# A selective scan, its projections and its convolution issued over twice as many elements, and the D * x term moved from TensorE to VectorE

## The chip, the core and the metric

One NeuronCore of a Trainium2 chip runs the whole program. The metric is the device time of one execution in microseconds (us). The engines named below are PE (TensorE, matrix multiply), DVE (VectorE), ACT (ScalarE), POOL (GpSimd) and SP (SyncE, which only issues DMAs here). Each works through its own instructions in order; semaphores tie them together.

## The reference

`x` is 8 sequences of 1024 tokens of 512 features, all float32. It is normalized, and two branches of the normalized `xn` are added to it:

```
xn  = layernorm(x)
out = x + mamba(xn) + ffn(xn)

mamba:  xb, z   = split(xn @ W_in)                        # 1024 channels each
        xc      = silu(causal_conv4(xb) + conv_b)         # depthwise, 4 taps
        B, C, d = split(xc @ W_x)                         # 16, 16, 1
        dt      = softplus(d + dt_bias)
        h_t     = h_{t-1} * exp(dt_t * A) + dt_t * xc_t * B_t      # 16 states a channel
        y_t     = sum over states(h_t * C_t) + D * xc_t
        result  = (y * silu(z)) @ W_out

ffn:    silu(q(xn) @ q(w_gate)) * (q(xn) @ q(w_up)), quantized, @ q(w_down)
```

Here `q` is a blockwise FP4 quantize and dequantize in blocks of 16, and the hidden width of `ffn` is 1408.

## The kernel before

**Chunks and slots.** Tokens are taken in chunks of `T` = 512: 16 chunks, two per sequence, so every even chunk starts from a zero state (`first`) and every odd one continues its neighbour and hands nothing on (`last`). The 1024 channels are 8 blocks `j` of 128. For the scan the 128 partitions hold 32 channels times 4 states, so a block is 4 quarters of channels (`NQ`), and the 16 states are 4 groups `q` (`NG`). A pair is one `(c, j, q, h)` with `h` the first of two neighbouring quarters: 64 pairs a chunk, 1024 in all. The loop in `sweep` gives each pair one slot.

**What one pair does.** `make_u` (L496): POOL multiplies `dt * x` by `B` for both quarters, 128x1024, into one of 3 `u` buffers, two slots ahead. `make_a` (L503): ACT computes `exp(dt * A)`, one instruction per quarter because the scale differs, into one of 2 PSUM buffers `ah`, one slot ahead. `scan` (L512): DVE runs the recurrence in place, one `tensor_tensor_scan` of 512 elements per quarter (L518), keeps the last column in `state` when the next chunk needs it (L524), and multiplies both quarters by `C` into one of 4 buffers `hc` (L526). Every two slots `sum_states` (L529) lets PE add the 4 states of a channel group into the PSUM bank `py`: 8 matmuls with the constant `summed`. At `q == 0` a 128x128 matmul with the diagonal `Dd` puts `D * xc` into `py` first (L535), with `xc` read back from DRAM as `xcr` (`fetch_x`, L546). After the last group `gate` (L555) multiplies `py` by `silu(z)`, read back as `zr` (`fetch_z`, L551).

**What runs beside it.** `sweep` (L821) fills PE with three other streams, written as generators that yield a cost in us: `ahead` (L471) prepares chunk `c + 1`, `finish` (L579) multiplies chunk `c - 1` by `W_out`, and `gate_up` (L600) or `downs` (L730) is the feed-forward. A credit per slot spreads the remaining cost evenly over the remaining slots, but for the last 12. The first sweep covers chunks 0 to 9 (640 slots) with `gate_up`, the second chunks 10 to 15 (384 slots) with `downs`. In both, the order on every engine is the order of the Python calls.

**Projection and convolution.** `project_x` (L337) multiplies 128 channels in two halves of 256 tokens, each with 3 tokens before it (259 columns, from an `xT` tile that holds 3 more tokens than the chunk), so that each half carries what its convolution needs. `convolve` reads the bank four times on ACT: one Identity with bias and scale (L351) and three scaled copies, `taps` (L357). `add` sums the taps on POOL (L363). `project_z` (L370) is 512 columns wide and is copied by ACT. `silus` (L386) follows when four halves are convolved; if they are not, it is put off by a slot.

**Work that follows later.** `later` (L272) puts an item into the list of a later slot, and `issue` (L279) takes the items of a slot in order. An item waits for the next slot if ACT work of `ENOUGH` = 2.0 us or more is already taken in this one, or if an item with the same key was put off.

**Banks.** Three PSUM banks (`p_mm`) serve all projections. They are used in a ring: `room` (L305) lets a new one start only if the last but two has had its reader issued:

```python
return whose in self.partly or len(self.banks) < 3 or not self.banks[-3][1]
```

The functions that the change touches:

Of the kernel before, what the change touches and what calls it, by code (L numbers as in the profile page):

```python
# [17 lines left out]
P = 128  # L18
# [6 lines left out]
LEAST = math.log(1.05 * 2.0**22)  # L25
T = 512
# [10 lines left out]
MOST = 6.0  # L37
TAIL = 12
# [47 lines left out]
class Net:  # L86
# [11 lines left out]
    def __init__(self, tc, ctx, x, W_in, conv_w, conv_b, W_x, A_log, D_param, dt_bias, W_out,  # L98
# [22 lines left out]
        self.p_mm = ctx.enter_context(tc.tile_pool(name="p_mm", bufs=3, space=PSUM))  # L121
# [35 lines left out]
        self.cb, self.dtb, Dp = vecs  # L157
# [12 lines left out]
        nc.vector.tensor_scalar(self.A, self.A, -1.0, None, ALU.mult)  # L170
# [7 lines left out]
        self.Dd = cpool.tile([P, J, P], F32, tag="Dd", name="Dd")  # L178
        for j in range(J):
            nc.vector.tensor_scalar(self.Dd[:, j, :], ident, Dp[:, j : j + 1], None, ALU.mult)  # L180
# [4 lines left out]
    def transposed(self, pp, src, n, name):  # L185
# [3 lines left out]
        for k0 in range(0, n, 4):  # L189
            kn = min(4, n - k0)  # L190
            pt = self.p_mm.tile([P, 4, P], F32, tag="mm", name=f"pt_{name}_{k0}")
            for k in range(kn):
                nc.tensor.transpose(pt[:, k, :], src[:, (k0 + k) * P : (k0 + k + 1) * P], self.ident)
            nc.scalar.copy(st[:, k0 : k0 + kn, :], pt[:, :kn, :])
        return st
# [83 lines left out]
    def issue(self):  # L279
# [3 lines left out]
        while self.due.get(self.now):  # L283
            item = work, bank, key, act = self.due[self.now].pop(0)
            if key in [i[2] for i in kept] or (act and used >= ENOUGH and self.timed):
                kept.append(item)
                continue
            used += act
            work()
            for b in bank or ():  # L290
                b[1] = False
# [7 lines left out]
    def bank(self, shape, name):  # L299
        assert self.room()  # L300
        b = [self.p_mm.tile(shape, F32, tag="mm", name=name), True]
        self.banks.append(b)
        return b

    def room(self, whose=None):  # L305

        return whose in self.partly or len(self.banks) < 3 or not self.banks[-3][1]
# [8 lines left out]
    def begin(self, c):  # L316
# [3 lines left out]
        H0 = self.H0  # L320
        s.xT = self.pool.tile([P, self.KM, H0 + T], F32, tag="xT", name=f"xT_{c}", bufs=1)
        if s.first:
            nc.gpsimd.memset(s.xT[:, :, :H0], 0.0)
        else:
            nc.sync.dma_start(s.xT[:, :, :H0], self.xnT_d[c - 1][:, :, T - H0 :])
        nc.sync.dma_start(s.xT[:, :, H0:], self.xnT_d[c])
        s.xc = self.pool.tile([P, self.J, T], F32, tag="xc", name=f"xc_{c}", bufs=1)
        s.z, s.xz_d, s.dd_d, s.reps = {}, [None] * self.J, [None] * self.J, [None] * self.J
        s.B, s.C, s.active, s.convolved = [None] * NG, [None] * NG, 0, 0
# [7 lines left out]
    def project_x(self, s, j, i, w):  # L337

        nc, c, H0 = self.nc, s.c, self.H0
        TH = T // 2  # L340
        b = self.bank([P, T], f"px_{c}_{j}_{i}")
        px = b[0]
        for k in range(self.KM):
            nc.tensor.matmul(  # L344
                px[:, : H0 + TH], w[:, k, :], s.xT[:, k, i * TH : i * TH + H0 + TH],
                start=(k == 0), stop=(k == self.KM - 1),
# [631 lines left out]
```

## Time and profile before

| | |
|---|---|
| median of 3 runs | 5353.9 us (5351.65 to 5355.68) |
| the profiled execution | 5357.3 us, of which the span of its instructions is 5355.5 us |
| preparation, up to the first scan | 0 to 537 us |
| first sweep, chunks 0 to 9 | 537 to 3745 us, 5.01 us a slot |
| second sweep, chunks 10 to 15 | 3745 to 5322 us, 4.11 us a slot |
| last output projection | 5322 to 5355 us |

Busy time is the time an engine spent in instructions; it overlaps between engines. A group of the profile lists a line, its engine, output <- inputs, the shape, the count, then busy us and the mean ns of one, then how long the engine stood idle just before such instructions and what ended that. The trace has two records for each float32 matmul of the program (one for each transpose). PEclk is the share of full speed that the clock of TensorE was granted. The ends of matmuls are modelled, so for them busy time divided by the count says more than the mean of one.

### The profile page before, as it was taken

How to read it: one execution, taken by the hardware profiler on the slowest of the kernel's cores; microseconds unless marked ns; L12 is line 12 of the kernel's file. 1: busy time of each engine (PE TensorE's matmuls, PEld its weight loads, DVE VectorE, ACT ScalarE, POOL GpSimd, SP SyncE). 2: the span in 40 equal slices, each digit the busy share in tenths (PEclk: the TensorE clock that was granted, in tenths of full speed). 3: DMA queues.
4: the chain of work that ended last, by engine and by line, in shares of the span. 5: the costliest groups of instructions: out<-in, count | busy, mean ns of one | idle time of the engine just before them, and what ended most of it. 6: DMA issues, size and time to landing. Idle time of an engine off the chain costs nothing.

```text
span 5355.5 us, 57041 instructions
## 1 busy us (share of the span) xinstructions
PE 4465.9 (83%) x17604; PEld 2529.2 (47%) x17604; DVE 4601.1 (86%) x5094; ACT 3312.6 (62%) x4829; POOL 4110.3 (77%) x2474
## 2 busy tenths in 40 slices
PE   3433788888898988989888998986998999899975
PEld 2322555564555556555555655654433343434321
DVE  3678789888898888788888888889899999899997
ACT  4665576766767577565767767576555565556532
POOL 6666788887888788787888988888677777778654
PEclk7765899999999999989999999998999999999986
DMA  5465557565665657556575665757586878587752
GB/s 158 142 206 155 148 172 192 148 193 153 178 185 154 188 139 204 152 161 177 162 201 157 190 176 157 192 148 212 156 241 162 228 194 236 160 229 195 220 128 57
DMA packets 635584, 937.83 MB, mean 175 GB/s; under 512 B 58624, under 2 KB 378112, under 8 KB 635152
## 3 DMA queue, kind: packets, MB, share of 16 engines
q1 hardware_dynamic: 624880, 931.66, 62.9%
q10 hardware_dynamic: 10400, 2.52, 0.2%
q8 instruction: 141, 2.31, 0.2%
q14 instruction: 163, 1.34, 0.1%
HBM read 676.81 MB, written 257.20 MB: 174 GB/s over the span
## 4 chain that ended last, share of the span: by engine, by line
PE 36%; DVE 31%; ACT 11%; POOL 8%; issue 8%; DMA 5%; SPq 1%; DVEq 0%; ACTq 0%; POOLq 0%
DVE ah L518 19%; PE pu L625 7%; PE po L589 6%; PE pod L748 6%; PE pg L625 5%; DVE hc L526 5%; PE pz L375 3%; ACT ah L507 3%; PE py L537 3%; POOL u L498 2%; PE px L344 2%; ACT L507 1%; POOL xc L363 1%; DVE pu L649 1%; PE ps L411 1%
## 5 line engine op out<-in xcount | busy, mean ns | idle before, releaser
L498 POOL TENSOR_TENSOR u<-rep,B 128x1024 f32<-128x1024 f32 x1024 | 2413.0, 2360 | 776.1 <-DVE ah L518 736.5
L507 ACT ACTIVATE ah<-rep,A 128x512 f32<-128x512 f32 x2048 | 1416.6, 692 | 1406.8 <-DVE hc L526 1359.3
L518 DVE TENSOR_TENSOR_SCAN ah<-ah,state,u 128x512 f32<-128x512 f32 x1024 | 1313.4, 1283 | 33.1 <-ACT ah L507 12.4
L526 DVE TENSOR_TENSOR hc<-ah,C 128x1024 f32<-128x1024 f32 x1024 | 1249.6, 1220 | 95.1 <-PE py L537 53.8
L518 DVE TENSOR_TENSOR_SCAN ah<-ah,u 128x512 f32<-128x512 f32 x1024 | 1254.0, 1225 | 44.2 <-ACT ah L507 21.6
L625 PE MATMUL pu<-wu,xq 128*128 128x256 f32 (+1 forms) x3072 | 683.9, 380 | 85.5 <-DVE h L640 25.3
L625 PE MATMUL pg<-wg,xq 128*128 128x256 f32 (+1 forms) x3072 | 661.0, 373 | 58.8 <-DMA wg<-gu 13.7
L537 PE MATMUL py<-hc,summed 128*32 128x512 f32 x4096 | 618.6, 629 | 80.8 <-DVE hc L526 80.5
L625 PEld LDWEIGHTS pu<-wu,xq 128*128 128x128 f32 x3072 | 564.5, 199 | 231.1 <-issue 29.3
L748 PE MATMUL pod<-dT,hTr 128*128 128x512 f32 x1408 | 637.6, 603 | 24.3 <-DMA hTr<-hT 19.0
L625 PEld LDWEIGHTS pg<-wg,xq 128*128 128x128 f32 x3072 | 557.0, 196 | 183.6 <-issue 74.8
L363 POOL TENSOR_TENSOR xc<-xc,taps 128x256 f32<-128x256 f32 x768 | 558.1, 727 | 82.5 <-ACT taps L357 42.3
L344 PE MATMUL px<-xT,wx 128*128 128x259 f32 x2048 | 530.1, 407 | 94.0 <-ACT h L636 47.9
L375 PE MATMUL pz<-xT,wz 128*128 128x512 f32 x1024 | 511.6, 646 | 71.1 <-ACT z L382 32.0
L344 PEld LDWEIGHTS px<-xT,wx 128*128 128x128 f32 x2048 | 393.9, 199 | 282.3 <-ACT taps L357 69.5
L589 PE MATMUL po<-Wout,y 128*128 128x512 f32 x1024 | 465.3, 607 | 13.5 <-ACT hT L678 10.0
L748 PEld LDWEIGHTS pod<-dT,hTr 128*128 128x128 f32 x1408 | 261.1, 191 | 398.5 <-issue 360.8
L375 PEld LDWEIGHTS pz<-xT,wz 128*128 128x128 f32 x1024 | 205.4, 207 | 330.3 <-issue 215.8
L589 PEld LDWEIGHTS po<-Wout,y 128*128 128x128 f32 x1024 | 192.5, 193 | 281.3 <-issue 262.6
L357 ACT ACTIVATE taps<-px,cw 128x256 f32<-128x256 f32 x768 | 305.5, 472 | 12.9 <-POOL xc L363 12.8
L640 DVE TENSOR_TENSOR h<-h,pu 128x512 f32<-128x512 f32 x192 | 121.8, 637 | 220.0 <-PE pu L625 216.5
L537 PEld LDWEIGHTS py<-hc,summed 128*32 128x32 f32 x4096 | 88.4, 109 | 437.6 <-issue 205.0
(107 smaller groups left out, 4482.1 us busy)
## 6 DMA issues: line engine op xcount, KB each, us to landing
rep<-ddd SPq DMA_DIRECT2D x512, 512.0 KB, 7.1
ddd<-dd SPq DMA_DIRECT2D x128, 512.0 KB, 4.4
hTr<-hT SPq DMA_DIRECT2D x64, 704.0 KB, 4.9
wg<-gu SPq DMA_DIRECT2D x80, 512.0 KB, 5.6
wu<-gu SPq DMA_DIRECT2D x80, 512.0 KB, 5.9
hT<-hT SPq DMA_DIRECT2D x80, 512.0 KB, 6.2
wx<-in_L_attn_W_in_dram SPq DMA_DIRECT2D x128, 256.0 KB, 2.8
wz<-in_L_attn_W_in_dram SPq DMA_DIRECT2D x128, 256.0 KB, 3.0
```

The source lines that it names most:

```text
L344: nc.tensor.matmul(px[:, : H0 + TH], w[:, k, :], s.xT[:, k, i * TH : i * TH + H0 + TH], start=(k == 0), stop=(k == self.KM - 1),)
L357: nc.scalar.activation(taps[:, k, :], px[:, k : k + TH], AF.Copy, scale=self.cw[:, j, k : k + 1])
L363: nc.gpsimd.tensor_tensor(ca, ca, taps[:, k, :], ALU.add)
L375: nc.tensor.matmul(b[0], w[:, k, :], s.xT[:, k, self.H0 :], start=(k == 0), stop=(k == self.KM - 1))
L498: self.nc.gpsimd.tensor_tensor(u, s.reps[j][:, h : h + 2, 1, :], s.B[q].unsqueeze(1).to_broadcast([P, 2, T]), ALU.mult)
L507: self.nc.scalar.activation(ah[:, i, :], s.reps[j][:, h + i, 0, :], AF.Exp, scale=self.A[:, g, q : q + 1])
L518: nc.vector.tensor_tensor_scan(ah[:, i, :], ah[:, i, :], u[:, i, :], 0.0 if s.first else self.state[:, g + i, q : q + 1], ALU.mult, ALU.add,)
L526: nc.vector.tensor_tensor(hc, ah, s.C[q].unsqueeze(1).to_broadcast([P, 2, T]), ALU.mult)
L537: nc.tensor.matmul(s.py[i * D4 : (i + 1) * D4, :], self.summed, hcs[i // 2][:, i % 2, :], start=False, stop=(q == NG - 1),)
L589: nc.tensor.matmul(b[0], s.y[:, j, i * P : (i + 1) * P], self.Wout[:, j, :], start=(j == 0), stop=(j == self.J - 1),)
L625: nc.tensor.matmul(b[0][:, i, :], xq[pair][:, k, i * P : (i + 1) * P], w[:, k, :], start=(k == 0), stop=(k == self.KM - 1),)
L748: nc.tensor.matmul(b[0], h[:, k, :], dT[:, k, :], start=(k == 0), stop=(k == self.KF - 1))
```

## The change

- **One scan per pair.** Both quarters go through one scan of 1024 elements. The decay at the first token of the second quarter must then be zero: `separate` (ACT) overwrites that `dt` with 1e30 so that its exp is 0, after it has computed that token's decay for all 4 groups into `carry`. For an odd chunk, `make_a` adds `carry * state` to the first element of the second quarter's `u` with one 128x1 Identity on ACT.
- **512 tokens at once.** `project_x` is one group of 4 matmuls of 512 columns. `convolve` reads its bank four times at 512 columns. `add` shifts the taps on POOL by slices; what reaches into the next chunk is kept in `over` and added there. `xT` no longer holds the 3 tokens before.
- **D * x at the gate.** DVE adds `xr * D` to `py` in place with `scalar_tensor_tensor`, ahead of the multiplication by `zr`. `Dd`, its matmul and `fetch_x` go; `fetch_xz` reads both `xr` and `zr` at the place where `zr` was read.
- **Any free bank.** The banks carry numbers; a new projection takes the one that was given back longest ago, in whatever order that came.
- Around these, `silus` and the copy of `z` return `AGAIN` when they are not ready and are then kept for the next slot; the keys of `add` and of the copy of `z` are their own. The costs that the sweep reckons with follow: 64 for `ahead` instead of 68, 1.1 for the first sum instead of 2.0.

The diff, cut to its core:

```diff
-        self.p_mm = ctx.enter_context(tc.tile_pool(name="p_mm", bufs=3, space=PSUM))
+        self.p_mm = ctx.enter_context(tc.tile_pool(name="p_mm", bufs=1, space=PSUM))
...
-        nc.vector.tensor_scalar(self.A, self.A, -1.0, None, ALU.mult)
+        nc.vector.tensor_scalar(self.A, self.A, -1.0, -SLOW, ALU.mult, ALU.min)
...
     def bank(self, shape, name):
-        assert self.room()
-        b = [self.p_mm.tile(shape, F32, tag="mm", name=name), True]
-        self.banks.append(b)
-        return b
+        i = self.frees.pop(0)
+        return [self.p_mm.tile(shape, F32, tag=f"mm{i}", name=name), i]
 
     def room(self, whose=None):
-        return whose in self.partly or len(self.banks) < 3 or not self.banks[-3][1]
+        return whose in self.partly or bool(self.frees)
...
+            if work() is AGAIN:
+                kept.append(item)
+                continue
             used += act
-            work()
             for b in bank or ():
-                b[1] = False
+                self.frees.append(b[1])
...
-    def project_x(self, s, j, i, w):
+    def project_x(self, s, j, w):
...
-                px[:, : H0 + TH], w[:, k, :], s.xT[:, k, i * TH : i * TH + H0 + TH],
-                start=(k == 0), stop=(k == self.KM - 1),
+                px, w[:, k, :], s.xT[:, k, :], start=(k == 0), stop=(k == self.KM - 1)
...
-            taps = self.pool.tile([P, H0, TH], F32, tag="dd", name=f"taps_{c}_{j}_{i}")
+            taps = []
             for k in range(H0):
-                nc.scalar.activation(
-                    taps[:, k, :], px[:, k : k + TH], AF.Copy, scale=self.cw[:, j, k : k + 1]
-                )
+                if k % 2 == 0:
+                    tile_ = self.pool.tile([P, 2, T], F32, tag="dd", name=f"taps_{c}_{j}_{k}")
+                taps.append(tile_[:, k % 2, :])
+                nc.scalar.activation(taps[k], px, AF.Copy, scale=self.cw[:, j, k : k + 1])
             def add():
+                over = self.over[:, j, :]
+                tt = nc.gpsimd.tensor_tensor
                 for k in range(H0):
-                    nc.gpsimd.tensor_tensor(ca, ca, taps[:, k, :], ALU.add)
+                    tt(ca[:, H0 - k :], ca[:, H0 - k :], taps[k][:, : T - H0 + k], ALU.add)
+                if not s.first:
+                    tt(ca[:, :H0], ca[:, :H0], over, ALU.add)
+                if not s.last:
+                    nc.gpsimd.tensor_copy(over, taps[0][:, T - H0 :])
+                    for k in range(1, H0):
+                        tt(over[:, : H0 - k], over[:, : H0 - k], taps[k][:, T - H0 + k :], ALU.add)
                 s.convolved += 1
-            self.later(1, add, key="a")
-        self.later(1, convolve, [b], "a", 2.2)
+            self.later(1, add, key="c")
+        self.later(1, convolve, [b], "a", 2.8)
...
         def copy():
+            if i == 0 and s.stored < h:
+                return AGAIN
...
-        self.later(1, copy, [b], "a", 0.6)
+        self.later(1, copy, [b], "z", 0.6)
...
-        if s.convolved < 4 * (h + 1):
-            self.later(1, lambda: self.silus(s, h), None, "a", 4.7)
-            return
+        if s.convolved < 2 * (h + 1) or s.copied < 2 * (h + 1):
+            return AGAIN
...
+    def separate(self, s, j):
+        nc = self.nc
+        if not s.first:
+            v = s.carry[j] = self.pool.tile(
+                [P, NQ // 2, NG], F32, tag="carry", name=f"carry_{s.c}_{j}"
+            )
+            for i in range(NQ // 2):
+                nc.scalar.activation(
+                    v[:, i, :], self.A[:, j * NQ + 2 * i + 1, :], AF.Exp,
+                    scale=s.reps[j][:, 2 * i + 1, 0, 0:1],
+                )
+        nc.scalar.copy(s.reps[j][:, 1::2, 0, 0], self.long)
...
     def make_a(self, s, j, q, h):
+        if q == h == 0:
+            self.separate(s, j)
...
+        if not s.first:
+            first = self.us[len(self.ahs)][:, 1, 0:1]
+            nc.scalar.activation(
+                first, self.state[:, j * NQ + h + 1, q : q + 1], AF.Identity, bias=first,
+                scale=s.carry[j][:, h // 2, q : q + 1],
+            )
...
-        for i in range(2):
-            nc.vector.tensor_tensor_scan(
-                ah[:, i, :], ah[:, i, :], u[:, i, :],
-                0.0 if s.first else self.state[:, g + i, q : q + 1],
-                ALU.mult, ALU.add,
-            )
+        a = ah.rearrange("p i t -> p (i t)")
+        nc.vector.tensor_tensor_scan(
+            a, a, u.rearrange("p i t -> p (i t)"),
+            0.0 if s.first else self.state[:, g, q : q + 1], ALU.mult, ALU.add,
+        )
...
-            nc.tensor.matmul(s.py, self.Dd[:, j, :], s.xcr, start=True, stop=False)
...
-        if q == 0 and j + 1 < self.J:
-            self.later(1, lambda: self.fetch_x(s, j + 1))
...
-        self.nc.vector.tensor_tensor(s.y[:, j, :], s.py, s.zr, ALU.mult)
+        v = self.nc.vector
+        v.scalar_tensor_tensor(s.py, s.xr, self.Dp[:, j : j + 1], s.py, ALU.mult, ALU.add)
+        v.tensor_tensor(s.y[:, j, :], s.py, s.zr, ALU.mult)
         if j + 1 < self.J:
-            self.later(1, lambda: self.fetch_z(s, j + 1))
+            self.later(1, lambda: self.fetch_xz(s, j + 1))
...
-        left = cost + len(now) // per * (29.0 + 68.0 + sums)
+        left = cost + len(now) // per * (29.0 + 64.0 + sums)
...
-                left -= 1.1 if pq else 2.0
+                left -= 1.1
```

## The prediction

> **What bounds the kernel now.** I read the busy shares first, then a table of engine times by stage, then what DVE and PE waited for in the first sweep, and last a stretch of the timeline where nothing but the scan is left. The page's totals:
>
> ```profile
> PE 4465.9 (83%) x17604; PEld 2529.2 (47%) x17604; DVE 4601.1 (86%) x5094; ACT 3312.6 (62%) x4829; POOL 4110.3 (77%) x2474
> ```
>
> No engine is full over the span. By stage (first sweep, second sweep, the end of the second without other PE work):
>
> ```profile
> 537.00:3745.00 3208.00, 2790.57 (x12248) 1788.57 (x12248) 2755.98 (x2944) 2144.47 (x3094) 2654.69 (x1596) 0.94 0.62 172
> 3745.00:5322.00 1577.00, 1436.34 (x4464) 574.77 (x4464) 1489.99 (x1468) 843.18 (x1285) 1109.11 (x661) 0.94 0.69 187
> 5180.00:5322.00 142.00, 65.25 (x154) 7.89 (x152) 135.89 (x113) 47.67 (x69) 78.02 (x34) 0.56 0.26 63
> ```
>
> Columns: stretch, length, PE, PEld, DVE, ACT, POOL, granted clock, DMA share, GB/s. The second sweep is DVE's: 1490 of 1577 us. In the first, DVE has 2756 and PE 2791 of 3208 us, and they wait for each other. DVE's waits there, and some of PE's:
>
> ```profile
> DVE h L640 <- PE pu L625: 216.5, 74, 28.5
> DVE r_False L576 <- PE po L589: 64.4, 20, 9.3
> DVE hc L526 <- PE py L537: 46.2, 22, 4.8
> DVE ah L518 <- ACT ah L507: 27.2, 28, 3.9
> ```
>
> ```profile
> PE px L344 <- ACT h L636: 47.9, 10, 8.9
> PE pth L675 <- ACT h L636: 40.9, 17, 9.2
> PE px L344 <- ACT taps L357: 37.3, 18, 7.0
> ```
>
> DVE stands for PE 335 us in all (the three rows and three of 4.1, 3.1 and 0.5), because PE is late with results that stand ahead of the next scan in DVE's order. PE stands some 310 us for readers (ACT mostly) that must empty a bank or finish an input. So DVE's work plus DVE's waits for PE make the first sweep, and DVE's work alone most of the second.
>
> **The scan.** At the end of the second sweep a slot is bare:
>
> ```profile
> 5256.48 1.23 DVE L526 TENSOR_TENSOR hc<-ah,C 128x1024 f32<-128x1024 f32 x1
> 5257.62 2.61 DVE L518 TENSOR_TENSOR_SCAN ah<-ah,state,u 128x512 f32<-128x512 f32 x2
> 5260.33 1.23 DVE L526 TENSOR_TENSOR hc<-ah,C 128x1024 f32<-128x1024 f32 x1
> ```
>
> Scan to scan is 3.86 us; two scans take 2.61 with `state`, and 2.50 in a zero-start chunk. These groups price the parts:
>
> ```profile
> L507 ACT ACTIVATE ah<-rep,A 128x512 f32<-128x512 f32 x2048 | 1416.6, 692 | 1406.8 <-DVE hc L526 1359.3
> L518 DVE TENSOR_TENSOR_SCAN ah<-ah,state,u 128x512 f32<-128x512 f32 x1024 | 1313.4, 1283 | 33.1 <-ACT ah L507 12.4
> L526 DVE TENSOR_TENSOR hc<-ah,C 128x1024 f32<-128x1024 f32 x1024 | 1249.6, 1220 | 95.1 <-PE py L537 53.8
> L518 DVE TENSOR_TENSOR_SCAN ah<-ah,u 128x512 f32<-128x512 f32 x1024 | 1254.0, 1225 | 44.2 <-ACT ah L507 21.6
> L344 PE MATMUL px<-xT,wx 128*128 128x259 f32 x2048 | 530.1, 407 | 94.0 <-ACT h L636 47.9
> L375 PE MATMUL pz<-xT,wz 128*128 128x512 f32 x1024 | 511.6, 646 | 71.1 <-ACT z L382 32.0
> ```
>
> No row has a scan of 1024. The step from 512 to 1024 elements is seen in `y` (L558, 128x512 out of PSUM, 682 ns) against `hc` (1220 ns): two short ones cost 2 x 682 - 1220 = 144 ns more than one long. A long scan is then 2 x 1225 - 144 = 2306 ns from zero, 0.19 us under 2.50, and 1283 + 1225 - 144 = 2364 ns with `state`, 0.25 under 2.61. Even and odd chunks are equal in number: 0.22 a slot. Bounds: nothing (all cost is by element), and 0.30, if the fixed part is a whole tiny copy (L524, 163 ns) besides the start from `state` (58 ns) and a gap of 0.08. A loss I leave out, since `hc` already crosses the same two banks in one instruction, its second 512 elements at 538 ns. I take 0.22, nearest to the `y` and `hc` rows: **141 us** off DVE in the first sweep (640 slots), **84** in the second (384); bounds 0 and 192, 0 and 115.
>
> **The gate.** One `scalar_tensor_tensor` of 128x512 per block comes to DVE. On two columns this form (L248, median 156 ns) costs what a copy does (163), so I take 0.70 from the `y` row; bounds 0.68 and 1.29 (the slowest row of 512, a scan). 80 blocks in the first sweep: +56 (54 to 103); 48 in the second: +34 (33 to 62). The single bank `py` is held 0.70 longer; the next block's first sum comes two slots later, so its cover is some 7 us of scans; without it PE would lose up to 90 us in all. `xr` is fetched eight slots ahead. The SP queue keeps the number of these reads; the eight small `xT` reads go.
>
> **PE.** `Dd` goes: group L535 is 140.2 us in 128 blocks, 1.10 each. Of the projections, 530.1 becomes 1024 records at `pz`'s 0.50 = 512, so 0.14 a block. First sweep 80 blocks: -99; second: -59. The weight loads that go ran beside matmuls: nothing. On PE alone this frees no time; it counts through DVE's waits. To size that I took the compiled order of both kernels, cut PE's list at each group of sums (512 stretches of two slots, 320 in the first sweep) and priced each stretch by busy time per matmul from the groups of before (`pg`, `pu` 0.43, `pz` 1.00, `po`, `pod`, `ps` 0.91, a sum 0.30, and so on). In the first sweep a stretch lasts 10.0 us on average; PE work beyond that is 368 us in all, close to DVE's 335 us of waits for PE (91%). Afterwards the first sweep's list is more even, since two halves became one group and banks come back in any order: stretches over 13.2 us fall from 45 to 14. At 9.5 us a stretch (where the sum below ends) the excess is 267, which at 91% is 243 us: **-92**. Bounds: 0, and -250 (PE's bank waits mostly gone). It leaves PE without other work in the last 20 slots of that sweep, where DVE sets the pace. In the second sweep DVE's waits for PE are 40 us, and the excess falls by a tenth: -4.
>
> The trace grants 0.94 of the clock in both sweeps but 0.56 where PE is busy 46%. [...]
>
> **ACT.** Convolution: six taps (305.5 / 768 = 0.40 each) and two L351 (0.55) are 3.5 us a block; three and one at 512 columns, 0.214 more each (`h` L636: 596 against 382 ns), are 2.6. Against 114 us saved stand 512 Identities of one element. The smallest row with one pointer operand is `rstd` (L243), 297 ns; a second pointer is 80 (L351 against L357): 0.38, so 193 us, and 128 `carry` and 128 copies at 0.30 at most: 77. Bounds for all of it: 0.1 each, as the 8 memsets on POOL (77 us), to 270. ACT stays near 64%, which costs nothing by itself. What counts is the time between `hc` and the next scan: the exps (1.42) begin 0.03 us after `hc`, and ACT stood 2.44 us idle ahead of them. With the Identity and a shorter scan some 2.1 us are left. Other ACT work between two exp pairs in excess of this is 323 us before (over 2.3) and 488 after in the first sweep, 82 and 128 in the second, by the same listing. Before, DVE waited 27 and 7 us for it, 8%. So **+14** and **+4**. The Identity also waits for POOL's `u`. Behind it stand the bank readers, for whom PE waits; but POOL itself waits 330 us for the scan to free `u` in that sweep, so it is ahead.
>
> **POOL.** Six adds at 727 ns become three near 1250 (L456): 78 us less. 256 tiny ones at 0.11 to 0.18 take back 28 to 47. It is covered by DVE; if not, it gains 30.
>
> **The sum.** First sweep -141 + 56 - 92 + 14 = -163, to 3045 us or 9.5 a stretch. Second -84 + 34 - 4 + 4 = -50. Preparation and the last projection: nothing. 5357.3 - 213 = 5144 for the profiled execution, which lies 3.4 above the median: **5140**.
>
> **The rivals.**
> 1. *The list's evenness is worth nothing*: DVE's waits for PE stay 335 us, since PE keeps waiting for ACT's long items. +92: 5232. For it: PE's waits name `h` and `hT` as often as `taps`. Chance 0.15.
> 2. *The banks were the whole obstacle*: DVE's waits fall to some 120 instead of 243: 5017. For it: 310 us of PE waits for readers. Against: many are for inputs, not for banks. 0.12.
> 3. *The scan costs the same per element*, so the change doesn't do what it says there. The second sweep loses its 84; in the first, slower stretches hide part (excess at 10.0 is 221, 201 of waits): 141 - 42 = 99. 5323. 0.08.
> 4. *Slower: ACT becomes what a scan waits for.* The convolution is one item of 2.6 us, past the 2.1 us of cover, where two of 1.75 fitted. If half of the excess of 616 us shows instead of 8%, +256: 5396. It decides from a share of 43% on. For it: in the second sweep DVE has little else to do meanwhile. Against: so far 34 of 405 us showed. 0.12.
>
> My forecast has 0.53. **Range** 5040 to 5370, which leaves out the fourth rival and half of the second, and takes in the scan's bounds. About 0.2% is what a measurement of this kernel can tell from no change: faster 0.85, same 0.03, slower 0.12.
>
> **What would show it.** One scan at 2.3 to 2.4 us and slots of 3.6 at the end of the second sweep; the gate's addition at 0.70; DVE's waits for PE in the first sweep near 240; DVE's waits for `ah` under 60. A first sweep near 3045 and a second near 1527 confirm the shares. Waits for `ah` over 250 us, or a long scan over 2.5 us, would make me wrong.

## The result and the profile after

The changed kernel takes **5283.3 us** (median of 4 runs, 5281.2 to 5304.8) against 5353.1 us for the kernel before on the same chip: a ratio of **0.9875** (95% interval 0.9859 to 0.9890). It is faster by 70 us, where 213 were forecast: the right side, a third of the size. The profiled execution took 5304.8 us, some 21 us above the other three; what a stage of it shows is good to about that, and comparisons of whole times below go by ratios.

The page's totals after; compare the counts with those of before:

```profile
PE 4385.3 (83%) x16324; PEld 2301.2 (43%) x16324; DVE 4498.5 (85%) x4191; ACT 3408.8 (64%) x5089; POOL 4041.0 (76%) x2338
```

The table by stage, cut (to 2 us) at the first scan, the scan of slot 640 and the last one (columns: stretch, length, then PE, PEld, DVE, ACT, POOL busy, granted clock, DMA share, GB/s). After:

```profile
0.00:568.00 568.00, 223.22 (x768) 144.14 (x768) 344.50 (x672) 323.06 (x423) 339.31 (x217) 0.64 0.51 156
567.00:3716.00 3149.00, 2726.42 (x11444) 1642.53 (x11444) 2686.58 (x2370) 2198.57 (x3252) 2610.55 (x1509) 0.93 0.63 175
3716.00:5268.00 1552.00, 1404.62 (x4048) 501.70 (x4048) 1463.55 (x1144) 888.19 (x1418) 1092.12 (x613) 0.93 0.71 191
```

And before, with the same three cuts, since the prediction's table began its first sweep 1 us later and ended it 11 us later:

```profile
0.00:536.00 536.00, 209.24 (x828) 153.07 (x828) 350.70 (x679) 323.94 (x450) 345.54 (x218) 0.68 0.56 165
536.00:3734.00 3198.00, 2790.31 (x12248) 1788.57 (x12248) 2746.25 (x2932) 2142.47 (x3091) 2650.48 (x1594) 0.94 0.62 172
3734.00:5320.00 1586.00, 1434.95 (x4462) 574.58 (x4460) 1500.44 (x1480) 846.18 (x1290) 1114.24 (x663) 0.94 0.69 188
```

The preparation is 32 us longer (forecast: nothing), the first sweep 49 shorter (163), the second 34 shorter (50). Read the first sweep as DVE's work and its waits. Work fell from 2746 to 2687. The waits of DVE after (what waited, for whom, total us, times, longest):

```profile
DVE h L671 <- PE pu L656: 176.6, 77, 25.3
DVE ah L553 <- ACT u L541: 76.4, 49, 11.8
DVE ah L553 <- ACT ah L535: 46.8, 33, 4.6
DVE r_False L607 <- PE po L620: 40.0, 23, 6.7
DVE hc L560 <- PE py L570: 35.1, 14, 6.4
```

For PE it waits 264 us (335 before, 243 forecast). For ACT it waits 137 us (31 before); 123 of them are ahead of a scan, where 27 stood before and 41 were forecast. Work and PE's part gave 131 us back; ACT took 106 of them again. The rest of the 49 us is mostly in pauses too short for the list of waits, which fell in all from 73 to 55 us, over 2932 instructions of DVE before and 2370 after.

The groups that answer to those of before:

```profile
L535 ACT ACTIVATE ah<-rep,A 128x512 f32<-128x512 f32 x2048 | 1415.9, 692 | 1139.1 <-DVE hc L560 1102.5
L560 DVE TENSOR_TENSOR hc<-ah,C 128x1024 f32<-128x1024 f32 x1024 | 1248.6, 1219 | 78.2 <-PE py L570 35.5
L553 DVE TENSOR_TENSOR_SCAN ah<-ah,state,u 128x1024 f32<-128x1024 f32 x512 | 1199.1, 2342 | 89.2 <-ACT u L541 88.2
L553 DVE TENSOR_TENSOR_SCAN ah<-ah,u 128x1024 f32<-128x1024 f32 x512 | 1169.4, 2284 | 65.2 <-ACT ah L535 60.4
L345 PE MATMUL px<-xT,wx 128*128 128x512 f32 x1024 | 491.1, 624 | 38.1 <-ACT h L667 21.4
```

The long scan is as priced (2342 and 2284 ns; 2364 and 2306 forecast). At the bare end of the second sweep, DVE on the timeline (start, us, instruction):

```profile
5247.77 1.23 DVE L560 TENSOR_TENSOR hc<-ah,C 128x1024 f32<-128x1024 f32 x1
5248.91 2.35 DVE L553 TENSOR_TENSOR_SCAN ah<-ah,state,u 128x1024 f32<-128x1024 f32 x1
5251.29 1.23 DVE L560 TENSOR_TENSOR hc<-ah,C 128x1024 f32<-128x1024 f32 x1
5252.43 2.35 DVE L553 TENSOR_TENSOR_SCAN ah<-ah,state,u 128x1024 f32<-128x1024 f32 x1
```

Scan to scan is 3.52 us against 3.86: the saving is there where nothing else runs. So the durations were right, and the loss is in how they make up a sweep.

One new stall stands out, the longest wait for `u`. The queue of ACT (in brackets: idle before, and its releaser):

```profile
2878.23 1.07 ACT L709 COPY hT<-pth 128x512 f32<-128x512 f32 x2 [0.84 <-DMA hT<-hT]
2893.17 0.59 ACT L392 COPY z<-pz 128x512 f32<-128x512 f32 x1 [13.86 <-DMA xz<-z]
2893.65 1.42 ACT L535 ACTIVATE ah<-rep,A 128x512 f32<-128x512 f32 x2
2895.01 0.37 ACT L541 ACTIVATE u<-state,u,carry 128x1 f32<-128x1 f32 x1
```

SP's queue in the same stretch, with a pause up to 2881 us ahead of a weight load for `px`:

```profile
2873.66 0.90 SPq L581 DMA_DIRECT2D zr<-xz  x1
2881.39 0.38 SPq L335 DMA_DIRECT2D wx<-in_L_attn_W_in_dram  x1
...
2883.33 1.16 SPq L409 DMA_DIRECT2D xz<-z  x1
...
2885.87 0.60 SPq L409 DMA_DIRECT2D xz<-z  x1
```

And DVE, which waits for what stands behind that copy on ACT:

```profile
2895.41 2.36 DVE L553 TENSOR_TENSOR_SCAN ah<-ah,state,u 128x1024 f32<-128x1024 f32 x1 [11.80 <-ACT u L541]
```

`z` has one buffer. Its next copy is in ACT's list once the store of the old content is issued by Python, but the store itself stands in SP's list behind the weight load, which stands for PE. ACT waits 13.9 us, the exps behind the copy come late, and DVE stands 11.8 us. Of the 13.9 us some 2 pass until the weight load is issued, 4.5 until the second store is, and 7.3 from there to the start of the copy: the queue is half of this stall and the transfer the other half.

### The profile page after: what moved, and what is told of

It is laid out like the page before. It is cut to its first block, busy times and chain, and to the rows that moved or that the text cites. A ratio compares the mean times of both kernels' runs of the same rounds, so it can differ in the third digit from the quotient of the medians.

```text
span 5302.8 us, 52505 instructions
## 1 busy us (share of the span) xinstructions
PE 4385.3 (83%) x16324; PEld 2301.2 (43%) x16324; DVE 4498.5 (85%) x4191; ACT 3408.8 (64%) x5089; POOL 4041.0 (76%) x2338
## 4 chain that ended last, share of the span: by engine, by line
PE 26%; DVE 21%; ACT 12%; DMA 5%; issue 4%; POOL 3%; SPq 0%; DVEq 0%; ACTq 0%; POOLq 0%
DVE ah L553 12%; PE po L620 8%; DVE hc L560 6%; PE pu L656 4%; PE pod L779 4%; ACT ah L535 4%; PE pg L656 3%; PE py L570 2%; PE pz L383 2%; PE px L345 2%; DMA rep<-ddd 2%; POOL u L523 1%; DMA xz<-z 1%; ACT L535 1%; ACT taps L359 1%
## 5 line engine op out<-in xcount | busy, mean ns | idle before, releaser
L553 DVE TENSOR_TENSOR_SCAN ah<-ah,state,u 128x1024 f32<-128x1024 f32 x512 | 1199.1, 2342 | 89.2 <-ACT u L541 88.2
L553 DVE TENSOR_TENSOR_SCAN ah<-ah,u 128x1024 f32<-128x1024 f32 x512 | 1169.4, 2284 | 65.2 <-ACT ah L535 60.4
L570 PE MATMUL py<-hc,summed 128*32 128x512 f32 x4096 | 648.8, 633 | 170.6 <-DVE hc L560 119.8
L656 PE MATMUL pu<-wu,xq 128*128 128x256 f32 (+1 forms) x3072 | 695.7, 384 | 102.5 <-ACT hT L709 63.5
L345 PE MATMUL px<-xT,wx 128*128 128x512 f32 x1024 | 491.1, 624 | 38.1 <-ACT h L667 21.4
L365 POOL TENSOR_TENSOR xc<-xc,taps 128x509 f32<-128x509 f32 (+2 forms) x384 | 440.6, 1147 | 52.9 <-ACT taps L359 34.1
L345 PEld LDWEIGHTS px<-xT,wx 128*128 128x128 f32 x1024 | 194.7, 198 | 315.5 <-issue 223.4
```

The source lines that it names most:

```text
L345: nc.tensor.matmul(px, w[:, k, :], s.xT[:, k, :], start=(k == 0), stop=(k == self.KM - 1))
L365: tt(ca[:, H0 - k :], ca[:, H0 - k :], taps[k][:, : T - H0 + k], ALU.add)
L553: nc.vector.tensor_tensor_scan(a, a, u.rearrange("p i t -> p (i t)"), 0.0 if s.first else self.state[:, g, q : q + 1], ALU.mult, ALU.add,)
L570: nc.tensor.matmul(s.py[i * D4 : (i + 1) * D4, :], self.summed, hcs[i // 2][:, i % 2, :], start=(q == 0), stop=(q == NG - 1),)
L656: nc.tensor.matmul(b[0][:, i, :], xq[pair][:, k, i * P : (i + 1) * P], w[:, k, :], start=(k == 0), stop=(k == self.KM - 1),)
```

## The experiments

The expectations letter the theories, in e1 to e4 as follows (e5, e13 and e14 say what their letters mean). A: work that ACT reaches too early (above all that copy of `z`) keeps the exps behind it. B: the added Identity and the longer convolution on ACT make the scans wait. C: the free choice of banks starts PE's groups in an order in which PE stands for `hT`. Against these stands the plainer one that later runs were made for: in a sweep where engines wait for each other, each passes on only a part of what it saves, and takes back a part of what is put on it. Stages are in us, of one profiled execution each; the last two columns are DVE's waits in the first sweep.

| run | ratio to before (95%) | preparation | first sweep | second | for PE | for ACT |
|---|---|---|---|---|---|---|
| before | 1 | 536 | 3198 | 1586 | 335 | 31 |
| after | 0.9875 (0.9859–0.9890) | 568 | 3149 | 1552 | 264 | 137 |
| e1 z in two buffers | 0.9809 (0.9792–0.9825) | 569 | 3115 | 1536 | 233 | 106 |
| e2 convolve later | 0.9915 (0.9895–0.9935) | 569 | 3163 | 1554 | 342 | 77 |
| e3 no Identity | 0.9817 (0.9794–0.9840) | 568 | 3112 | 1541 | 237 | 102 |
| e4 ring of banks | 0.9971 (0.9958–0.9983) | 568 | 3192 | 1550 | 331 | 111 |
| e5 two scans | 1.0016 (1.0005–1.0026) | 571 | 3157 | 1605 | 200 | 70 |
| e6 matmul for D * x | 0.9790 (0.9765–0.9814) | 570 | 3126 | 1526 | 297 | 138 |
| e7 before + free banks | 0.9938 (0.9924–0.9953) | 592 | 3108 | 1591 | 239 | 51 |
| e8 e1 + carry on POOL | 0.9795 (0.9775–0.9815) | 569 | 3107 | 1545 | 232 | 65 |
| e9 pooled banks in preparation | 0.9835 (0.9819–0.9850) | 546 | 3134 | 1546 | 256 | 126 |
| e10 no D * x | 0.9816 (0.9799–0.9833) | 570 | 3122 | 1528 | 264 | 145 |
| e11 e6 + e9 | 0.9766 (0.9748–0.9784) | 550 | 3118 | 1529 | 289 | 133 |
| e12 e11 + store from ACT | 0.9733 (0.9717–0.9749) | 545 | 3103 | 1526 | 284 | 128 |
| e13 less work on PE | 0.9804 (0.9789–0.9819) | 561 | 3111 | 1541 | 228 | 117 |
| e14 less work on ACT | 0.9832 (0.9813–0.9852) | 572 | 3112 | 1542 | 250 | 117 |
| e15 convolution alone | 0.9937 (0.9922–0.9951) | 552 | 3160 | 1572 | 257 | 76 |
| e16 scan alone | 0.9932 (0.9916–0.9949) | 537 | 3187 | 1561 | 395 | 91 |

A difference of two ratios is turned into us with 5355, before's time; it is uncertain by some 12 us. A stage is less certain than that: e9 leaves the sweeps as they are after, and its profile has 3134 and 1546 us for them, 15 and 6 less than after's.

**e1, `z` in two buffers.**

```diff
-                s.z[h] = self.pool.tile([P, 2, T], F32, tag="z", name=f"z_{c}_{h}", bufs=1)
+                s.z[h] = self.pool.tile([P, 2, T], F32, tag="z", name=f"z_{c}_{h}", bufs=2)
```

> The changed kernel with a second buffer for z, so that ACT's copy of the next z need not wait until the store of the last one has left. Theory A (ACT stands in its queue behind that store: 104 us in the first sweep against 45 before, and the exps behind it come late): the waits of the copy for the store go from 133 us to under 10, DVE's waits for ACT's exps and Identities from 148 us to about 100, the time from 5283 to about 5240. Theory B (the extra Identity and the long convolution are what makes the scans wait): the copy's waits go, DVE's waits for ACT stay near 148 us and the time within 10 us of 5283. Theory C (the banks given out in any order make PE wait for the hT copies): within 10 us of 5283 as well.

35 us faster than after (0.9809 against 0.9875). Waits of ACT in the first sweep, in e1:

```profile
ACT ah L535 <- DVE hc L560: 523.5, 226, 9.8
ACT xc L351 <- PE px L345: 99.4, 40, 5.9
ACT h L667 <- PE pg L656: 97.0, 45, 5.2
ACT z L392 <- PE pz L383: 54.7, 21, 4.8
```

The row `ACT z L392 <- DMA xz<-z`, 104.5 us after, is gone. The stall is real and worth 35 us, no more: DVE still waits 106 us for ACT. Not all of it is new: the row that answers to it before (L382) has 45.2 us in the first sweep.

**e2, the convolution a slot later.**

```diff
-        self.later(1, convolve, [b], "a", 2.8)
+        self.later(2, convolve, [b], "a", 2.8)
```

> The changed kernel with the convolution put two slots behind its projection instead of one, so that ACT doesn't reach it before PE has finished a group that is now twice as long (ACT's waits there rose from 36 to 82 us in the first sweep). If these waits hold up the exps (a second form of theory A): the waits go under 30 us, DVE's waits for ACT fall by about 30 and the time to about 5250. If they don't matter (theories B and C): 5275 to 5300, since a bank is held a slot longer.

21 us slower than after. In the first sweep ACT's wait for `px` fell from 82 to 4 us and DVE's for ACT from 137 to 77, but the bank is held a slot longer, and PE stood for it (first sweep of e2):

```profile
PE pz L383 <- ACT taps L359: 90.4, 27, 7.3
```

In this run the late reader cost more through PE (DVE's waits for it rose by 78 us) than it saved through ACT (60).

**e3, without the Identity.** The one-element addition in `make_a` is left out (`first = ...` and the activation behind it).

> The changed kernel without the Identity that adds the carried state to the second quarter: odd chunks lose the state of every second quarter, so a part of the computation is left out. Theory B: DVE's waits for ACT fall from 148 us to under 80 and the time to about 5220. Theory A: only 0.37 us less on ACT in every second chunk's slots, about 15 us off: 5265 to 5283.

31 us faster; ACT is 148 us less busy in the two sweeps. A quarter of the waits for ACT goes, not all: 137 became 102.

**e4, the ring again.**

```diff
-        i = self.frees.pop(0)
+        i = self.turn % 3
+        self.turn += 1
+        self.frees.remove(i)
...
-        return whose in self.partly or bool(self.frees)
+        return whose in self.partly or self.turn % 3 in self.frees
```

> The changed kernel with its three banks given out in a ring again, a new projection waiting until the next bank in turn has its reader issued. Theory C: PE's waits for the hT copies fall from 112 us in the first sweep to about 30 and the time falls, to about 5250. If the free choice is a gain instead, as the prediction's -92 had it together with the wider groups: DVE's waits for PE rise from 266 us in the first sweep by 40 or more, and the time to 5320 or above.

51 us slower than after. PE's waits for `hT` stayed (106 us; 117 after, 33 before), so the free choice is not what brings most of them, and theory C falls. They go with the convolution's part: 83 us in e15 below, which has the ring and two scans, and 20 in e16. The free choice is a gain.

**e5, two scans.** The loop of two `tensor_tensor_scan`s is put back; `separate` and the Identity go.

> The changed kernel with two scans of 512 per pair again, without the decay set to zero, the carry and the Identity. Theory A (the long scan saves DVE 0.2 us a slot as predicted, and the Identity that it needs on ACT gives some 30 us of it back): DVE is busy some 195 us more, its waits for ACT fall from 162 to about 110, and the time rises from 5283 by 110 to 160, to about 5410. Theory B (the scan's gain is hidden behind PE and ACT in the first sweep): the time rises by less than 60, mostly in the second sweep. The preparation stays near 568 us if the scan has no part in its 31 us.

75 us slower than after, and no faster than before. The stages say where, in e5's windows:

```profile
571.00:3728.00 3157.00, 2729.81 (x11444) 1643.14 (x11444) 2803.45 (x3010) 2084.81 (x2772) 2611.97 (x1509) 0.93 0.63 174
```

In the first sweep DVE has 117 us more work than after, and the sweep is 8 us longer (23 against e9's): DVE's waits for PE and ACT are 270 us in place of 401. The second is 53 us longer (59 against e9's). The 75 us lie between what the two theories gave.

**e6, the matmul for D * x.** `Dd`, its matmul and `fetch_x` are put back; the `scalar_tensor_tensor` goes.

> The changed kernel with D * x added by the diagonal matmul again, xc read back on its own, and the sweep reckoning with that cost as before. DVE loses 95 us of work, PE gains 140. If the term is worth what the prediction's steps say (first sweep: DVE -56, PE's later results some +45; second sweep: DVE -34): the time falls by 20 to 50, to about 5245, which would make this part of the change a loss. If PE is what the first sweep waits for: it rises by 20 to 60. The preparation stays near 568 us if Dd has no part in its 31 us.

45 us faster than after. The part of the change that moves this work to DVE is a loss.

**e7, the kernel before with free banks.** Only `bank`, `room` and what returns a bank are changed.

> The kernel before with nothing but the new rule for banks: three numbered banks, the one that was given back longest ago taken. From the run with the ring (1.0% slower than the changed kernel): DVE's waits for PE in the first sweep fall from 335 us to about 280 and that sweep by 50 us. Preparation: if numbered banks are what makes it 31 us longer, it goes from 536 to about 567 and the whole time stays near 5335; if the wider projection in the preparation does it, the preparation stays at 536 and the time goes to about 5305.

33 us faster than before, as expected (5335), but by larger steps than expected; its first two stages:

```profile
0.00:592.00 592.00, 243.88 (x844) 165.61 (x844) 355.68 (x678) 335.27 (x461) 350.01 (x221) 0.65 0.51 150
```

```profile
592.00:3700.00 3108.00, 2755.60 (x12232) 1767.59 (x12232) 2745.93 (x2931) 2139.41 (x3087) 2645.13 (x1591) 0.95 0.64 177
```

The first sweep is 90 us shorter with the same work on DVE: its waits for PE fell by 96. The preparation, whose order isn't written by hand, is 56 us longer.

**e8, e1 with the carry on POOL.** `separate` multiplies `carry` by `state` and `make_a` adds it, both with `gpsimd.tensor_tensor` in place of the Identity.

> The changed kernel with two buffers for z, and with the carried state added to u by POOL: one product of carry and state per block and one addition of one element per pair, in place of the Identity on ACT. If the two runs' gains add (0.66% by the second buffer, 0.58% without the Identity): about 5220. If POOL's tiny additions (0.19 us each, 107 us in all) come too late for the scan or hold up u: 5255 or above, with DVE's waits for POOL up from 5 us to 40 or more.

The same as e1 (0.9795 against 0.9809). DVE's waits for ACT fell by 41 us in the first sweep, but its waits for POOL became 68 (5 or less after): the wait moved with the work.

**e9, the preparation's banks from a rotating pool.**

```diff
+        if not self.timed:
+            return [self.p_mm.tile(shape, F32, tag="mm", name=name), None]
...
-        with tc.tile_pool(name="prep", bufs=2) as pp:
+        with (
+            tc.tile_pool(name="prep", bufs=2) as pp,
+            tc.tile_pool(name="prep_mm", bufs=3, space=PSUM) as self.p_mm,
+        ):
```

> The changed kernel, but in the preparation the banks come from a pool with three buffers of one name, as before, and the numbered ones begin with the first sweep. In the kernel before, free banks by number went with a preparation of 592 us instead of 536. Theory (the numbers fix the order in which the preparation's transposes take the banks): it goes from 568 to about 537, the sweeps stay, the time goes to about 5252. Rival (the wider projection or the convolution makes the preparation longer): it stays above 560 and the time near 5283.

21 us faster than after, and the preparation is 22 us shorter:

```profile
0.00:546.00 546.00, 215.56 (x776) 149.46 (x776) 353.48 (x671) 323.68 (x421) 343.14 (x218) 0.67 0.55 162
```

The numbered banks cost most of the preparation's 32 us, though not all of it, as the theory had it.

**e10, no D * x at all.** The `scalar_tensor_tensor` is left out.

> The changed kernel without D * x at all: the addition at the gate is left out, and no matmul takes its place; what is read for it is still read. Against the run with the matmul (0.85% faster than the changed kernel) this prices the matmul. If PE's 140 us of it lie in slots where PE has nothing else to do: the same time as there, within 10 us of 5240. If the first sweep runs at PE's pace: 5210 or below, DVE's waits for PE under those of the run with the matmul (328 us in both sweeps).

32 us faster than after; e6, which computes the term with a matmul, is no slower than this. Second sweep of both, e6 first:

```profile
3696.00:5222.00 1526.00, 1416.41 (x4142) 513.85 (x4144) 1427.89 (x1096) 888.20 (x1416) 1093.40 (x613) 0.95 0.72 194
```

```profile
3692.00:5220.00 1528.00, 1394.27 (x4046) 499.86 (x4048) 1428.10 (x1096) 887.81 (x1416) 1092.31 (x613) 0.94 0.72 194
```

PE is 22 us busier there in e6, and the sweep is not longer. The first sweeps, e6 first:

```profile
570.00:3696.00 3126.00, 2762.62 (x11604) 1653.44 (x11604) 2630.54 (x2292) 2198.06 (x3252) 2611.46 (x1509) 0.95 0.65 176
```

```profile
570.00:3692.00 3122.00, 2724.46 (x11444) 1641.85 (x11444) 2630.30 (x2292) 2198.00 (x3252) 2609.95 (x1509) 0.93 0.64 177
```

By before's 1.10 us a block the term's matmuls are an estimated 88 us there, but PE is only 38 us busier, at a granted clock of 0.95 in place of 0.93. Over the whole run the seven costliest groups of matmuls, the same in number in both, took 57 us less in e6, and 24 of these are the sums into `py` (618.8 against 642.9). Whether that helps e6's time isn't separated.

**e11, e6 and e9 together.**

> The changed kernel with D * x by the diagonal matmul and with the preparation's banks from the pool. If the two gains add (0.85% and the 31 us of the preparation): about 5210. If the shorter preparation only moves a wait into the first sweep: 5235 or above.

5231.0 us: 58 faster than after, where the two alone gave 45 and 21; within the uncertainty the two add.

**e12, and `z` stored from ACT's queue.**

```diff
-                nc.sync.dma_start(d[:, 1, :], z[:, i, :])
+                nc.scalar.dma_start(d[:, 1, :], z[:, i, :])
```

> As the run with the matmul and the preparation's banks from the pool, and z is stored by a DMA that ACT issues itself right behind the silu, instead of one at the end of SP's queue. If the copy of the next z waited for SP's queue more than for the transfer: its waits go from some 115 us to under 40, DVE's waits for ACT fall by 30 or more, and the time goes to about 5180. If it waited for the transfer, or if issuing costs ACT as much: within 10 us of that run.

5212.5 us, 18 faster than e11 and 143 faster than before: the fastest version here. But the waits of the `z` copy for the store fell in the first sweep only from 76 to 53 us (105 after), which is more than was expected to be left, and DVE's waits for ACT fell by 5 us where 30 or more were expected. So the gain is measured, but neither its way nor what holds the transfer now is shown.

**e13, e14: less work on one engine.** In e13 `project_z` sums two of its four matmuls. In e14 one scaled copy is made and used for all three taps.

```diff
-        for k in range(self.KM):
+        for k in range(2):
```

> The changed kernel with half of the projection of z left out (two of its four matmuls, so z is wrong): PE loses 160 us of work in the first sweep and 80 in the second, in the same order and with the same waits. Theory A (the first sweep goes at PE's pace, so that what DVE saves there turns into waits): the first sweep shortens by 100 or more from 3149 us, DVE's waits for PE fall from 264 to under 180. Theory B (it goes at the pace of ACT's queue, which DVE and PE both wait for): by less than 40, and DVE's waits for ACT rise. Second sweep: within 15 us of 1552, since DVE bounds it.

> The changed kernel with two of the three scaled copies of each convolution left out (the first one is added three times, so the convolution is wrong): ACT loses 98 us in the first sweep and 49 in the second. Theory B: the first sweep shortens by 60 or more, with DVE's waits for ACT (137 us there) and PE's for ACT's readers both down. Theory A: by less than 25. If both this and the run with less work on PE shorten it by a third to two thirds of what was taken away, no engine sets the pace alone.

First sweeps, e13 and then e14:

```profile
561.00:3672.00 3111.00, 2614.56 (x11120) 1591.18 (x11120) 2686.06 (x2370) 2196.90 (x3249) 2611.28 (x1509) 0.92 0.64 177
```

```profile
572.00:3684.00 3112.00, 2719.82 (x11440) 1641.33 (x11440) 2685.69 (x2370) 2109.83 (x3089) 2610.25 (x1509) 0.93 0.64 177
```

Both first sweeps are some 37 us shorter than after's (22 than e9's), and each expectation missed: e13 is far from the 100 us of its theory A, and DVE's waits for ACT fell where its theory B had them rise; e14 lies between its theories, or by e9's sweep just inside its theory A. Neither engine alone sets the pace. With e3 and e10 they make a price list against after, by busy time in the two sweeps and by ratios of the whole:

| run | taken off | faster by | per us |
|---|---|---|---|
| e10 | DVE 91 us | 32 us | 0.35 |
| e13 | PE 156 us | 38 us | 0.24 |
| e3 | ACT 148 us | 31 us | 0.21 |
| e14 | ACT 130 us | 23 us | 0.18 |

Each "faster by" is uncertain by some 12 us, so the order of the engines is not shown; that none passes on all, and that ACT and PE pass on something, is.

**e15, the convolution alone:** after with e4, e5, e6 and e9 in it, so that the wide projection and convolution (with the new keys, AGAIN and the costs that the sweep reckons with) are what is left.

> The wider projection and convolution (with the new keys and AGAIN) as the only part: two scans, the matmul for D * x, the ring of banks, and the preparation's banks from the pool. By the prediction's terms (PE -11 us in the first sweep, ACT -114 in all, fewer but longer items) it would be worth 0 to 40 us. From the sum of the other parts as the runs show them (scan -75, gate +45, free banks -60 in the first two of these orders, numbers in the preparation +20 to +31, all together -70) some 10 us: 5345. Its preparation should be near 540 us; if it is above 560, the wider projection and not the numbers makes it longer.

34 us faster than before: 38 off the first sweep, 14 off the second, 16 onto the preparation, whose 552 us lie between the two forecasts. The stall of the `z` copy is in this part, as ACT's waits over the whole run show (133.4 us after):

```profile
ACT z L398 <- DMA xz<-z: 127.6, 32, 10.6
```

**e16, the scan alone:** the kernel before with the long scan, `separate` and the Identity.

> The kernel before with nothing but the long scan and what it needs (separate, carry, Identity). Taken out of the changed kernel, the scan was worth 75 us, of which 8 in the first sweep, though DVE was 117 us less busy there. If the first sweep hides it whatever the rest is like: the same here, first sweep within 20 us of 3196, second shorter by 50 to 60, the time near 5285. If it was hidden only because the other parts had already taken the slack: the first sweep shortens by 80 or more and the time goes to 5220.

36 us faster than before. Its two sweeps:

```profile
537.00:3724.00 3187.00, 2780.99 (x12246) 1782.82 (x12248) 2629.71 (x2291) 2255.97 (x3572) 2652.44 (x1594) 0.94 0.64 172
3724.00:5285.00 1561.00, 1428.26 (x4464) 575.03 (x4460) 1428.49 (x1096) 919.35 (x1578) 1114.64 (x663) 0.94 0.73 191
```

DVE has 117 us less in the first and 72 less in the second, ACT 113 and 73 more. The first sweep is 11 us shorter, the second 25. What DVE saved in the first it waits, as its waits there show:

```profile
DVE h L669 <- PE pu L654: 250.0, 95, 27.0
DVE r_False L605 <- PE po L618: 71.4, 26, 9.3
DVE hc L555 <- PE py L566: 62.2, 39, 5.5
DVE ah L548 <- ACT u L536: 47.5, 41, 4.0
DVE ah L548 <- ACT ah L530: 37.0, 29, 5.2
```

60 us more for PE (335 to 395) and 60 more for ACT (31 to 91): together the 117 saved. The first theory is right on the first sweep; the second sweep gained half of the 50 to 60 us that it gave. With the price list, 188 us off DVE at 0.35 and 187 onto ACT at 0.2 give 29 us; 36 were measured.

## Why the prediction was wrong

**The step that failed** is "So DVE's work plus DVE's waits for PE make the first sweep, and DVE's work alone most of the second", used with the waits as something that DVE's own speed leaves alone, and with it "ACT stays near 64%, which costs nothing by itself". The first holds roughly as a sum on before's trace (2746 and 335 of 3198 us); it is no rule for what a saving does. When DVE is faster it comes earlier to results of PE and ACT that are no earlier, and waits. The scan alone (e16) saved what was forecast on DVE within a sixth (188 of 225 us) and the kernel gained 36: the rest came back as waits, half for PE and half for ACT, which had been given as much work as DVE lost. ACT's new work is, by these runs, the smaller part of the loss: without the Identity the changed kernel is 31 us faster (e3), and DVE work taken off with nothing put on ACT passed on 0.35 (e10).

The steps, in us over both sweeps unless said otherwise:

| step | forecast | measured, by |
|---|---|---|
| scan, with ACT's extra work | -225 + 18 | -36 built alone (e16); -75 as the last part (e5) |
| addition at the gate | +90 | +32 (e10) to +45 (e6) |
| PE's list: banks and wide projection | -96 | -85 banks (e7), -52 convolution (e15) |
| copy of `z` ahead of its store | not seen | in e15's -52; +35 at most (e1) |
| preparation | 0 | +32 |
| sum, with e16 for the scan | -213 | -96 to -109; the kernel: -70 |

The measured column adds runs made on different kernels, and rows for e7 and e15 leave out their preparations, which the row below has. Built alone, the parts gain 26 to 39 us more than together; which of them overlap isn't shown, except that the banks are worth less as the last part (51, e4). The first row is the one that misses most, by either run.

**Scan.** Durations right (2.28 and 2.34 us, slot 3.52 against 3.6). Its worth was mis-sized by 171 us (132 by e5), for the reason above. In the second sweep, which I called DVE's, its 72 us became 25: DVE's waits grew by 46 us, from 48 to 94, half for PE and half for ACT.

**Gate.** 0.75 us where 0.70 was taken. It passed on a third to a half. That the matmul it replaced cost PE 1.10 us a block didn't matter: putting it back lost nothing against leaving the term out (e6, e10).

**PE's list.** "-92" was near in size: DVE's waits for PE fell by 71 us. But e7, which only frees the banks, takes 90 us off the first sweep; I had put it down to both parts together, and the convolution alone takes 38 off that sweep and 14 off the second. That the evenness of the list is the reason isn't shown. PE's work itself fell by 64 us in the first sweep where 99 were listed. As the last part added, the banks are worth 51 (e4).

**ACT.** "+14" became 106 of waits in the first sweep, and DVE's waits for `ah`, named as a sign to stay under 60 us, were 123. 8% of the listed excess was taken to show; by 137 + 25 us of waits against 616 it is about a quarter. The cover of 2.1 us was also too high for odd chunks, where the prediction's own numbers give 2.44 - 0.25 - 0.38 = 1.81; at the bare end of after ACT stands 1.80 to 1.87 us ahead of the exps, 3.19 where a gate lies between. The fourth rival named the mechanism, with its threshold at 43%. Removing the Identities (e3), or the stall of the copy (e1), gets back 31 and 35 us; moving them to POOL gets nothing that can be told from none (e8: 7 us).

**The `z` copy** I had not followed. By the code, its key before kept it behind other ACT items that were put off, and by then the store had more often left (45 us of such waits in the first sweep, 104.5 after). Given its own key it comes up earlier, while the store still stands in SP's queue or is on its way. No run changes that key alone.

**Preparation.** "Nothing" was wrong: numbered banks cost 22 us of it (e9) and what is left of it goes with the wide projection's part (e15 is 16 above before without them; e9, e11, e12 and e15, whose banks there come from the pool, lie at 545 to 552). Why that part costs there is open.

**Rivals.** The first (waits for PE stay 335) and the third (scan by element) are false: 264, and 2.3 us. The second is false. That the result lies inside the range is luck: it got there by a cause that only the fourth touched, and the gate and PE's list came out 45 to 58 and 41 us better than forecast, against the scan's 171.

The clock: PE's mean went from 0.94 to 0.93 in both sweeps. In the first sweeps it is 0.92 where PE is busy for 84% of the time (e13), 0.93 and 0.94 at 87% (after and before), and 0.95 at 88 and 89% (e6 and e12): lower where PE is busy less, and these runs don't separate which brings the other. As an estimate, by proportion, 0.01 of clock is 29 us of PE's 2726, worth 7 at PE's price above. Over the whole run of e13 the `pz` matmuls took 280 us in place of 513, but PE's total fell by only 160 (4385.3 to 4225.8): the other groups, the same in number, took some 73 us more. So in e13 a part of what was taken off PE came back.

## What to carry to other kernels

Where several engines wait for one another in fixed orders, don't price a saving at its full length, and don't call work on an engine that is 64% busy free: here a microsecond was worth some 0.35 on DVE, 0.24 on PE and 0.2 on ACT, each give or take 0.1, so that work moved from one engine to another at equal length brings little (188 us for 36 in e16). Before an item is allowed to come earlier, look at what it waits for and in whose queue that stands; and build the parts of a change one by one, since here two of them were losses (the addition at the gate, numbered banks in the preparation) inside a gain, and without them and with the `z` store moved the kernel is at 0.9733.

## What was not expected of the hardware

Over a whole run no engine comes near full use (85% for DVE and 83% for PE after). In the second sweep of e12, the fastest version, DVE does come to 94% (1428 of 1526 us), but in its first sweep DVE has 85% and PE 89%:

```profile
545.00:3648.00 3103.00, 2757.90 (x11606) 1655.93 (x11608) 2629.91 (x2291) 2196.18 (x3250) 2609.52 (x1509) 0.95 0.64 178
```

The rest of DVE's time there is mostly waits, 284 us for PE and 128 for ACT.

One-element work is far from free on ACT and POOL: the Identity of one element takes 372 ns on ACT against 692 for 512 elements of exp, and the tiny operations with `over` on POOL (1 to 3 columns) take 186 to 195 ns in the mean. A scan has a fixed part too: 2 x 1225 - 2284 = 166 ns are saved by joining two. On POOL an addition of 512 columns shifted by one to three took from 1087 ns (509 and 510 elements) to 1268 ns (511); the runs don't say why.
